# Query and key projection without padding, score banks read in pairs, and sums spread over the gaps, in a kernel of three attention blocks

## The chip, the cores and the metric

The kernel runs on one core of a Trainium2 chip. The metric is the device time in microseconds (us). A profile of one execution stands beside the timed runs; its times are microseconds from the start of the span, unless marked ns. TensorE multiplies matrices (PE in the profile, PEld for its weight loads), VectorE is DVE, ScalarE is ACT, GpSimd is POOL, and SyncE (SP) issues most of the transfers.

## What is computed

Input `x` has 4 sequences of 512 tokens with 288 features; a condition vector per sequence gives shifts, scales and gates. Three transformer blocks follow one another: block 0 with a mixture of four experts, block 1 with a dense part, then a rotation of a 64-dimensional subspace, then block 3 with a dense part. All is float32. The attention is the same in all three: 16 heads of 18 features.

```python
qkv = (h @ w_qkv + b_qkv).reshape(B, N, 3, nh, hd).transpose(2, 0, 3, 1, 4)
q, k, v = (qkv[0], qkv[1], qkv[2])
attn = jax.nn.softmax(jnp.einsum('bhqd,bhkd->bhqk', q, k) * hd ** (-0.5), axis=-1)
o = jnp.einsum('bhqk,bhkd->bhqd', attn, v).transpose(0, 2, 1, 3).reshape(B, N, C)
x = x + g_msa[:, None, :] * (o @ w_proj + b_proj)
```

Block 3 has no bias on q, k and v. After each attention come a second normalisation and the experts or the dense part (288 to 1152 to 288).

## The kernel before, in words

**Stages.** The code runs `attention(0)`, the experts, `attention(1)`, a dense part, `rotate()`, `attention(3)`, a dense part (L2018 to L2053). In the profile the tiles of the attentions begin with `a0`, `a1` and `a3`. Beside the attentions and the experts run background pieces, a step per `tick()` (L770): reflections (an orthogonal basis, on VectorE with small transfers `v<-pT`), a matrix exponential, and the routing of tokens to experts.

**Groups.** One attention is 16 groups `r` of one sequence and four heads (L786). Heads are padded from 18 to 32 rows, so the four heads of a group fill the 128 partitions of a query tile `qks[r, 0]` and a key tile `qks[r, 1]`. The weights come padded from the host; `queries_and_keys` (L829) multiplies padded weight columns with the activations `hT` (two full feature chunks and a remainder of 32 rows), one bank for the queries and one for the keys, and ScalarE adds the bias on the way out (L856). The key bias holds a 1 in row 18 of each head and the query row 18 is 0.

**Scores twice.** `row_max` (L862) makes the scores of 128 query tokens of one head with all 512 keys in a PSUM bank, and VectorE reduces them to the row maximum (L873). When a group has all its maxima, `shift` (L913) transposes them on TensorE and subtracts them from the query tile: row 18 of each head is then minus the maximum, which the 1 in the key's row 18 adds to every score. `weight` (L875) makes the scores again, transposed and shifted, and ScalarE takes Exp (L885). `sums` (L898) multiplies these with the values, which carry a column of ones, into one bank `av`; a key tile of 128 tokens is four products, one for each head.

**Gaps.** The order of TensorE is written out by hand: `mm` (L75) ties each product to the one before. A group runs through eight gaps `k` (L1143). A gap starts with `quad` (L888): two row-maximum products of group `r` and two weight products that lag nine gaps behind, on the four different 32-row strips of the array. Then come listed background steps, the sums (two key tiles in gap 1, two in gap 5, L1147 to L1152), and pieces of jobs by a string per gap (`pieces`, L1042): Q is a product of the next group's projection, A a block of transposed activations for the next sequence, X a values or output product. The last gap ends with `shift`. Groups 3, 4, 13 and 14 have no X. The first group's maxima run in four opening rounds (L1130).

**Banks and buffers.** PSUM has eight banks: four of tag `sc` for scores, three of tag `de` for everything else, and `av` (L64). The banks of the score ring come round in the order of `quad`, so a row-maximum bank is used again in the next gap, after its maximum has been read. Query and key tiles are rings of three, weights `p` a ring of ten (L1107). `Feed.hidden` (L1253) uses the score banks in the dense and expert parts: four remainder products into four banks, then the main ones.

**Transfers.** `collect` (L943) spreads a group's sums over partitions with copies on POOL's queue (L962) and one on SP (L957); `invert` (L964) sends the reciprocals on SP. Weights of an attention are loaded by `attention_weights` (L238): for block 0 at the program's start, for block 1 during the experts, for block 3 after attention 1. `Experts.loads` (L1441) lists copies of the expert weights in DRAM, issued from attention 0. `beside_of` and `in_turn` (L98, L102) order an instruction after the last one that was recorded for its engine; apart from such ties an engine's order is set by a scheduler from what is ready.

## Time and profile before

| what | value |
|---|---|
| median of 3 runs | 2056.34 us (2051.73 to 2058.46) |
| profiled execution | 2033.07 us |
| its span, first to last instruction | 2031.4 us |
| mean granted TensorE clock | 0.983 |
| attention 0, first score product to last sums | 29.9 to 412.9 |
| attention 1, the same | 936.9 to 1303.0 |
| attention 3, the same | 1507.5 to 1865.6 |
| VectorE busy in 80 to 386 (attention 0) | 222.7 of 306 |
| VectorE busy in 1507 to 1845 (attention 3) | 208.5 of 338 |

How to read the lines: a group line has the code line, the engine, the operation, written tile and read tiles, shapes and count; then busy time, the mean of one in ns, and the engine's idle time just before, with what ended it. In a timeline line stand the start, the length, the engine, the line, the operation and the count that was merged; `[0.76 <-DVE max L873]` is idle time and what ended it. A float32 product appears as two instructions, so one score product is two MATMUL records. Matmul lengths overlap in the pipeline, so the distance between starts is what one costs.

### The profile page before, as it was taken

What the parts mean: (1) busy time and instruction counts of PE and PEld (TensorE: products, weight loads), DVE (VectorE), ACT (ScalarE), POOL (GpSimd) and SP (SyncE); (2) the same over time, 40 slices, a digit from 0 to 9 for tenths busy, and PEclk for the clock granted to TensorE, in tenths of its full rate; (3) what the DMA queues carried; (4) which work ended last, traced back from release to release, by engine and by line L of the source; (5) the groups of instructions that cost most, each with busy time, mean ns of one, the idle gap of its engine ahead of it and who ended that gap; (6) DMA issues with size and microseconds to landing.
All of it is one profiled execution on the core that took longest, in us unless ns stands there. A gap on an engine that the chain in (4) does not pass through costs nothing.

```text
span 2031.4 us, 29536 instructions
## 1 busy us (share of the span) xinstructions
PE 1957.2 (96%) x10932; PEld 1045.6 (51%) x10932; DVE 1074.3 (53%) x3103; ACT 765.4 (38%) x1409; POOL 569.2 (28%) x803
## 2 busy tenths in 40 slices
PE   7999999999999999999999999999999999999998
PEld 4434444466667777776434443456654344433565
DVE  5666777623454333446777877454255556554211
ACT  1545555333312232322555544421125455555220
POOL 3111221443434446651332122211401111213101
PEclk9989999899999999999999999999999899999999
DMA  7421111447655766751112111220000111111000
GB/s 152 119 52 20 23 33 34 106 121 222 180 155 163 223 191 206 220 183 30 45 42 43 33 39 40 47 69 19 21 1 10 28 29 35 28 27 23 18 16 22
DMA packets 95698, 155.89 MB, mean 77 GB/s; under 512 B 33571, under 2 KB 71310, under 8 KB 95554
## 3 DMA queue, kind: packets, MB, share of 16 engines
q0 software_dynamic: 28672, 89.90, 14.7%
q1 hardware_dynamic: 66770, 64.10, 13.8%
q8 instruction: 86, 1.41, 0.3%
q14 instruction: 58, 0.48, 0.1%
q10 hardware_dynamic: 112, 0.01, 0.0%
HBM read 125.29 MB, written 18.48 MB: 71 GB/s over the span
## 4 chain that ended last, share of the span: by engine, by line
PE 70%; DVE 7%; DMA 4%; POOL 1%; issue 1%; ACT 1%; SPq 0%; POOLq 0%; DVEq 0%; ACTq 0%
PE e0h L76 9%; PE e0o L76 8%; PE a3m L76 7%; PE a1m L76 6%; PE av L76 6%; PE a3psqk L76 4%; PE f1h L76 4%; PE f3h L76 4%; PE a1psqk L76 4%; PE f1o L76 3%; DVE max L873 3%; PE f3o L76 3%; DMA v<-pT 2%; DMA wr<-in_wrot 1%; PE a3psv L76 1%; PE a3pp L76 1%
## 5 line engine op out<-in xcount | busy, mean ns | idle before, releaser
L873 DVE TENSOR_REDUCE max<-a3m 128x1 f32<-128x512 f32 x256 | 164.6, 686 | 132.9 <-PE a3s L76 122.3
L76 PE MATMUL e0h<-e0hT,e0w 128*128 128x256 f32 (+1 forms) x1188 | 229.0, 404 | 4.9 <-DMA e0w<-w1c,wrow 4.2
L873 DVE TENSOR_REDUCE max<-a0m 128x1 f32<-128x512 f32 x256 | 165.3, 683 | 94.3 <-PE a0s L76 81.7
L873 DVE TENSOR_REDUCE max<-a1m 128x1 f32<-128x512 f32 x256 | 165.8, 684 | 75.0 <-PE a1s L76 68.4
L76 PE MATMUL e0o<-e0w,e0hm 128*128 128x288 f32 x756 | 201.6, 417 | 0.0
L76 PEld LDWEIGHTS e0h<-e0hT,e0w 128*128 128x128 f32 (+1 forms) x1188 | 166.2, 189 | 62.3 <-issue 37.1
L885 ACT ACTIVATE a0p<-a0s 128x512 f32<-128x512 f32 x256 | 140.2, 596 | 146.8 <-PE a0s L76 146.7
L885 ACT ACTIVATE a1p<-a1s 128x512 f32<-128x512 f32 x256 | 140.9, 596 | 142.4 <-PE a1s L76 142.1
L885 ACT ACTIVATE a3p<-a3s 128x512 f32<-128x512 f32 x256 | 140.0, 596 | 139.2 <-PE a3s L76 139.1
L76 PE MATMUL a1m<-a1qk,a1qk 32*128 32x512 f32 x512 | 159.2, 647 | 8.0 <-DVE max L873 6.9
L76 PE MATMUL a0m<-a0qk,a0qk 32*128 32x512 f32 x512 | 159.4, 647 | 6.4 <-DVE max L873 5.3
L76 PEld LDWEIGHTS e0o<-e0w,e0hm 128*128 128x128 f32 x756 | 141.9, 192 | 42.5 <-issue 4.0
L76 PE MATMUL a0s<-a0qk,a0qk 32*128 32x512 f32 x512 | 160.4, 655 | 1.3 <-DVE max L873 1.3
L76 PE MATMUL a1s<-a1qk,a1qk 32*128 32x512 f32 x512 | 159.8, 647 | 0.2 <-DVE u L547 0.2
L76 PE MATMUL a3m<-a3qk,a3qk 32*128 32x512 f32 x512 | 152.1, 647 | 6.8 <-DVE max L873 5.5
L76 PE MATMUL a3s<-a3qk,a3qk 32*128 32x512 f32 x512 | 153.5, 647 | 0.3 <-DVE a3qk L927 0.3
L1279 ACT ACTIVATE e0hm<-e0h,e0w 128x256 f32<-128x256 f32 x189 | 89.5, 473 | 166.7 <-PE e0h L76 166.7
L607 POOL TENSOR_TENSOR nrm<-n,phalf 64x1 f32<-64x1 f32 (+31 forms) x64 | 36.6, 573 | 297.9 <-DVE n L604 294.1
L1813 ACT COPY e0r<-e0o 128x288 f32<-128x288 f32 x44 | 17.5, 398 | 184.1 <-PE e0o L76 176.4
L76 PEld LDWEIGHTS a1m<-a1qk,a1qk 32*128 32x128 f32 x512 | 47.4, 184 | 72.8 <-DVE max L873 44.1
L76 PEld LDWEIGHTS a0m<-a0qk,a0qk 32*128 32x128 f32 x512 | 47.4, 185 | 67.9 <-DVE max L873 38.8
L76 PE MATMUL f1h<-f1hT,w 128*128 128x512 f32 (+1 forms) x216 | 80.8, 614 | 0.4 <-ACT f1hT L502 0.4
(465 smaller groups left out, 3270.0 us busy)
## 6 DMA issues: line engine op xcount, KB each, us to landing
eo<-e0r SPq DMA_DIRECT2D x44, 144.0 KB
ada<-in_ada SPq DMA_DIRECT2D x18, 324.0 KB
wr<-in_wrot SPq DMA_DIRECT2D x16, 288.0 KB
g<-gates SPq DMA_DIRECT2D x24, 144.0 KB
w1c<-in_w SPq DMA_DIRECT2D x20, 144.0 KB
w<-in_w SPq DMA_DIRECT2D x6, 432.0 KB
x<-in_x SPq DMA_DIRECT2D x16, 144.0 KB
w1c<-in_w SPq DMA_DIRECT2D x8, 288.0 KB
```

Of the source, the lines that this page charges most:

```text
L76: ins = nc.tensor.matmul(*args, **kwargs).ins
L607: in_turn("POOL", nc.gpsimd.tensor_tensor(nrm, n2, phalf[0:n], ALU.pow))
L873: take("DVE", nc.vector.tensor_reduce(m[:, t, i, D : D + 1], ps, AX.X, ALU.max))
L885: take("ACT", nc.scalar.activation(p, ps, AF.Exp, scale=D**-0.5))
L1279: nc.scalar.activation(self.hms[i][f], ps[r][:, 0 : self.width], func, bias=b1(f)),
L1813: take("ACT", nc.scalar.copy(y, ps))
```

## The change

- **Projection.** Weights hold 576 columns without padding, ordered head by head with the query and the key of a head side by side. A column chunk is seven units of 18 (126 columns), five chunks per sequence. `queries_and_keys` makes one chunk per group (two where the next group is a sequence's first), in halves of 256 tokens and two `de` banks, into a tile `u`. Then eight transfers, four on SP for the queries and four on POOL for the keys, copy each head's 18 rows to its padded place.
- **Tiles.** The three query and three key tiles stay for the whole attention; POOL sets them at its start. Since the query's row 18 still holds an old maximum, `row_max` reads 18 rows, and `shift` multiplies by a mask before it subtracts.
- **Weights.** For block 0 the padded weights are loaded to other tiles and ScalarE copies them together. For blocks 1 and 3 twelve transfers in attention 0 compact them in DRAM. The bias goes through DRAM in three transfers that depend on one another.
- **Scores.** The score banks are two tiles of two banks. Two heads' scores go to one tile, and one reduction or one Exp reads both banks. `hidden` takes its banks in the same way.
- **Order.** One key tile is summed in gap 3, 5, 7 and in gap 1 of the next group but one; the strings are written anew; the first half of the first sequence's values is made before the opening rounds.

```diff
+UC = HC * D
+NU = -(-2 * H // HC)
...
-    banks = {"sc": 4, "de": 3}
-
     def bank(tag, name):
-        return psum.tile([P, 512], F32, tag=tag, name=name, bufs=banks[tag])
+        return psum.tile([P, 512], F32, tag=tag, name=name, bufs=3)
+
+    def two_banks(name):
+        return psum.tile([P, 2, 512], F32, tag="sc", name=name, bufs=2)
...
+    mask = cst.tile([P, 1], F32, tag="mask", name="mask")
+    nc.vector.tensor_reduce(mask, ident[:, D::DP], AX.X, ALU.add)
+    nc.vector.tensor_scalar(mask, mask, -1.0, 1.0, ALU.mult, ALU.add)
...
+        def step(l, k, n):
+            to = compact[l][:, k, :].rearrange("p (h s d) -> s p h d", s=2, d=D)[n]
+            src = a[f"wqk{l}"][:, k, n * NG * P : (n + 1) * NG * P]
+            src = src.rearrange("p (h e) -> p h e", e=DP)[:, :, 0:D]
+            beside_of("SP", nc.sync.dma_start(to, src))
+
+        return [
+            lambda l=l, k=k, n=n: step(l, k, n)
+            for l in (1, 3)
+            for k in range(KC)
+            for n in range(2)
+        ]
...
+        def biases():
+            load(w["bqk"], a[f"bqk{l}"])
+            wide = dram.tile([2 * NG * P], F32, tag=f"bw{l}", name=f"bw{l}")
+            load(wide.rearrange("(j p) -> j p", p=P), a[f"bqk{l}"].rearrange("p j -> j p"))
+            flat = dram.tile([2 * C], F32, tag=f"bu{l}", name=f"buf{l}")
+            load(
+                flat.rearrange("(h s d) -> h s d", s=2, d=D),
+                wide.rearrange("(s h e) -> h s e", s=2, e=DP)[:, :, 0:D],
+            )
+            full = 2 * C // UC
+            load(w["bu"][:, 0:full], flat[0 : full * UC].rearrange("(c p) -> p c", p=UC))
+            load(w["bu"][0 : 2 * C - full * UC, full:NU], flat[full * UC :].unsqueeze(1))
...
         def qk():
-            load(w["bqk"], a[f"bqk{l}"])
-            full_chunks(w["qk"], a[f"wqk{l}"])
+            biases()
+            if compact:
+                full_chunks(w["qk"], compact[l])
+                return
+            for n in range(2):
+                t = wt.tile([P, W1R], F32, tag="w1", name=f"wide{l}_{n}", bufs=4)
+                t = t[:, 0 : MC * NG * P].rearrange("p (m n) -> p m n", m=MC)
+                full_chunks(t, a[f"wqk{l}"][:, :, n * NG * P : (n + 1) * NG * P])
+                heads = t.rearrange("p m (h e) -> p m h e", e=DP)
+                for m in range(MC):
+                    o = apart(w["qk"], n)
+                    in_turn("ACT", nc.scalar.copy(o[:, m], heads[:, m, :, 0:D]))
...
             def queries_and_keys(r):
...
+                b, g = groups[r]
+                for c in range(g + 1 if g else 0, g + 2):
+                    yield
+                    m = min(UC, 2 * C - c * UC)
+                    cols = slice(c * UC, c * UC + m)
+                    ps = [bank("de", f"{name}psqk{r}_{c}_{k}") for k in range(2)]
+                    tokens = [slice(k * T // 2, (k + 1) * T // 2) for k in range(2)]
+
+                    def product(k, n, rows):
+                        mm(
+                            ps[k][0:m, 0 : T // 2],
+                            lhsT=w["qk"][:, n, cols] if n < MC else w["qkr"][rows, cols],
+                            rhs=hTs[b][rows, n, tokens[k]],
+                            start=(n == MC),
+                            stop=(n == MC - 1),
+                        )
+
+                    for k in range(2):
+                        product(k, MC, slice(k * RR, (k + 1) * RR))
+                    u = us[b, c] = pool.tile([P, T], F32, tag="u", name=f"{name}u{r}_{c}")
+                    for k in range(2):
+                        for n in range(MC):
+                            yield
+                            product(k, n, slice(0, P))
+                        nc.scalar.activation(
+                            u[0:m, tokens[k]],
+                            ps[k][0:m, 0 : T // 2],
+                            AF.Identity,
+                            bias=w["bu"][0:m, c : c + 1],
+                        )
+
+                for i in range(GH):
+                    for s, queue in ((0, nc.sync), (1, nc.gpsimd)):
+                        c, row = divmod(2 * (g * GH + i) + s, HC)
+                        o = qks[r, s][i * DP : i * DP + D, :]
+                        queue.dma_start(o, us[b, c][row * D : (row + 1) * D, :])
+
+            def heads_rows(i, n=DP):
+                return slice(i * DP, i * DP + n)
+
+            def row_max(r, t, i):
+
+                m = maxima[r % 2].rearrange("p t (h d) -> p t h d", d=DP)
+                ps = two_banks(f"{name}m{r}_{t}_{i}")
+                for k in range(2):
+                    mm(
+                        ps[:, k, :],
+                        lhsT=qks[r, 0][heads_rows(i + k, D), t * P : (t + 1) * P],
+                        rhs=qks[r, 1][heads_rows(i + k, D), :],
+                        start=True,
+                        stop=True,
+                    )
+                    yield
+                take(
+                    "DVE",
+                    nc.vector.tensor_reduce(m[:, t, i : i + 2, D], ps, AX.X, ALU.max),
+                )
...
+            def weight(r, t, i):
+                s = two_banks(f"{name}s{r}_{t}_{i}")
+                for k in range(2):
                     mm(
-                        ps[s],
-                        lhsT=w["qkr"][rows, g * P : (g + 1) * P],
-                        rhs=hTs[b][rows, MC, :],
+                        s[:, k, :],
+                        lhsT=qks[r, 1][heads_rows(i + k), t * P : (t + 1) * P],
+                        rhs=qks[r, 0][heads_rows(i + k), :],
                         start=True,
-                        stop=False,
+                        stop=True,
                     )
...
-                p = pool.tile([P, T], F32, tag="p", name=f"{name}p{r}_{t}_{i}", bufs=tags["p"])
-                take("ACT", nc.scalar.activation(p, ps, AF.Exp, scale=D**-0.5))
-                return p
+                    yield
+                p = pool.tile([P, 2, T], F32, tag="p", name=f"{name}p{r}_{t}_{i}", bufs=tags["p"])
+                take("ACT", nc.scalar.activation(p, s, AF.Exp, scale=D**-0.5))
+                for k in range(2):
+                    ps[r, t, i + k] = p[:, k, :]
+                yield
...
+                halves = [what(r, n // 2, n % 2 * 2) for what, r, n in halves]
+                for _ in range(3):
+                    for half in halves:
+                        next(half)
...
                 q = qks[r, 0]
-                take("DVE", nc.vector.tensor_sub(q, q, ps))
+                take(
+                    "DVE",
+                    nc.vector.scalar_tensor_tensor(q, q, mask, ps, ALU.mult, ALU.subtract),
+                )
...
-                pieces = {0: "QQ", 2: "QQQ", 3: "QQQ", 4: "XQX", 6: "XX", 7: "X"}
+                pieces = {0: "QQ", 1: "Q", 2: "QQ", 4: "XX", 5: "X", 6: "XX"}
+                if g == NG - 1:
+                    pieces = {0: "QQQ", 1: "Q", 2: "QQQ", 3: "Q", 4: "QQ", 5: "X", 6: "XXX", 7: "X"}
...
-                    pieces = {0: "QQA", 2: "QQQ", 3: "QQQ", 4: "QAA", 6: "XXX", 7: "XX"}
+                    pieces = {0: "QQQ", 1: "Q", 2: "QA", 3: "A", 4: "A", 5: "XX", 6: "XXX"}
...
-            tags = {"qk0": 3, "qk1": 3, "p": 10}
+            tags = {"p": 5}
+            n, gaps = len(groups), 2 * NT
...
+            for k in range(3):
+                for s in range(2):
+                    t = pool.tile([P, T], F32, tag=f"qk{s}_{k}", name=f"{name}qk{s}_{k}", bufs=1)
+                    if s == 0:
+                        nc.gpsimd.memset(t, 0.0)
+                    else:
+                        nc.gpsimd.tensor_copy(t, w["bqk"][:, NG : NG + 1].to_broadcast([P, T]))
+                    for r in range(k, n, 3):
+                        qks[r, s] = t
...
-            first = [queries_and_keys(0)]
+            first = [queries_and_keys(0), values(0, 0)]
...
-            jobs["X"], jobs["Y"] = values(0, 0), values(0, 2)
+            jobs["X"] = values(0, 2)
...
-            for t, pieces in enumerate(("QQQQ", "QQQQQ", "XXXXX", "YYYYY")):
+            for t, pieces in enumerate(("QQ", "QQQ", "XX", "XXX")):
...
                     if k == 1 and r > 1:
-                        sums(r - 2, 2)
-                        sums(r - 2, 3)
-                    if k == 5:
-                        sums(r - 1, 0)
-                        sums(r - 1, 1)
+                        sums(r - 2, NT - 1)
+                    if k % 2 and k > 1:
+                        sums(r - 1, k // 2 - 1)
...
-                if k == 0:
-                    sums(n - 2, 2)
-                    sums(n - 2, 3)
+                if k == 1:
+                    sums(n - 2, NT - 1)
...
-            ps = [bank("sc", f"{self.name}h{i}_{f}") for i, f in chunks]
+            ps = []
+            for k in range(0, len(chunks), 2):
+                two = two_banks(f"{self.name}h{chunks[k][0]}_{chunks[k][1]}")
+                ps.extend(two[:, n, :] for n in range(2))
...
-            got = [lambda: features(self.wg[:, :, 0:E], a["wgate"])]
+            got = [lambda: features(self.wg[:, :, 0:E], a["wgate"])] + compacting()
```

## The prediction

> **What bounds the kernel now.** First the page's busy line, then the groups, then the timeline of a few gaps, because an average over the span does not say which wait ends last.
>
> ```profile
> PE 1957.2 (96%) x10932; PEld 1045.6 (51%) x10932; DVE 1074.3 (53%) x3103; ACT 765.4 (38%) x1409; POOL 569.2 (28%) x803
> ...
> L873 DVE TENSOR_REDUCE max<-a3m 128x1 f32<-128x512 f32 x256 | 164.6, 686 | 132.9 <-PE a3s L76 122.3
> ...
> L76 PE MATMUL a3m<-a3qk,a3qk 32*128 32x512 f32 x512 | 152.1, 647 | 6.8 <-DVE max L873 5.5
> ```
>
> TensorE is busy almost throughout, and the score products wait only 5.5 us for the maxima in the whole third attention. I call the work from one block of four score products to the next a gap; a group of four heads has eight, numbered 0 to 7. The timeline of gap 2 in group 2 of the third attention (start, length in us):
>
> ```profile
> 1553.99 0.69 PE L76 MATMUL a3m<-a3qk,a3qk 32*128 32x512 f32 x1
> ...
> 1555.06 1.56 PE L76 MATMUL a3psqk<-a3hT,wqk 128*128 128x256 f32 x6
> 1555.14 1.29 DVE L873 TENSOR_REDUCE max<-a3m 128x1 f32<-128x512 f32 x2 [1.27 <-PE a3s L76]
> ...
> 1556.55 0.69 PE L76 MATMUL a3m<-a3qk,a3qk 32*128 32x512 f32 x1
> ```
>
> The four score products share the array and take 1.07 (1553.99 to 1555.06), three projection pieces 1.49, so 0.497 each, and the gap is their sum, 2.56: TensorE-bound. The same reading gives 0.92 for the sums of one key tile, 0.585 for a values or output product, 0.87 for the shift's four transposes. A gap with nothing to fill it shows the second bound:
>
> ```profile
> 1583.12 0.69 PE L76 MATMUL a3m<-a3qk,a3qk 32*128 32x512 f32 x1
> ...
> 1584.28 1.29 DVE L873 TENSOR_REDUCE max<-a3m 128x1 f32<-128x512 f32 x2 [2.21 <-PE a3s L76]
> ...
> 1585.02 0.69 PE L76 MATMUL a3m<-a3qk,a3qk 32*128 32x512 f32 x1 [0.76 <-DVE max L873]
> ```
>
> Products to maximum 1.16, the first maximum 0.686, release to the next product 0.06: 1.90. This loop is the floor of a gap, because a score bank is filled again one gap later; the other gaps lie above it.
>
> **The change, part by part.**
>
> Projection (gain on TensorE). A group needs 8 pieces of 0.497 and a pair of remainder products (0.96): 4.94 us, 79 per attention. After: five column chunks per batch, each 4 pieces and a remainder pair half as long (0.48): 2.47 each, 49 per attention. So 30 us of TensorE time go per attention, 89 in all. That is the gain only if nothing else ends the gaps.
>
> Paired banks (new floor). One maximum now reads two banks, and the next pair of products needs both. The trace has no such read. A VectorE read of 256 columns from PSUM takes 418 ns, one of 512 686: 1.047 ns a column, so 1.22 for 1024. Bounds: 1.07 (the slope alone) and 1.37 (two old ones); the slope's value is nearest to its rows, so I take 1.22. The floor rises from 1.90 to 1.16 + 1.22 + 0.06 = 2.44. The paired Exp, 596 ns plus 427 more at ScalarE's slope (687 for 512 columns, 473 for 256), is 1.02: its loop, 2.25, lies under VectorE's.
>
> Sums in every other gap. Nothing is saved; 1.84 in gaps 1 and 5 becomes 0.92 in gaps 1, 3, 5, 7. An ordinary group (third attention, group 6) measures 2.55, 2.91, 2.56, 2.56, 2.66, 2.91, 2.24, 2.76 = 21.2. After: gaps 0 and 2 hold 1.07 + 0.98, under the floor, 2.44; gap 1 1.07 + 0.92 + 0.5 = 2.49; gaps 3, 4, 6 2.44; gap 5 2.58; gap 7 with the shift 2.86: 20.1. TensorE's own work in it would be 18.6, and the floor holds five gaps up by 1.5 in all, so 1.1 of the saving arrives. The other kinds, in the same way: with activations 22.0 to 21.3; with two chunks 21.4 to 21.2 (20.8 to 20.3 without output products); without values 20.7 to 19.9. Over groups 1 to 14 of the third attention: 12.5 us.
>
> The first two attentions have other VectorE work, 111 and 113 us against 48 (reflections, routing). VectorE's free time in a 2.44 gap is 2.44 - 1.22 = 1.22, and a step of the reflections takes about 1.3. From score product to score product their groups 1 to 14 already take 310 and 306 against the third's 299 (4 us of a clock event left out of the first and the third). To the third's new 287 I add one and a half times that excess, 303 and 297: gains 7 and 9. Sum of the gaps: **-28.5**.
>
> Copies to padded tiles (new wait). Per group four copies on SP and four on POOL, like `oo<-raw` (0.51 to issue on POOL, 1.9 to land) and `den<-raw` (0.63 on SP): 2.5 + 1.9 = 4.4 after the last bias. In a running group they start after gap 2 (gap 4 with two chunks), 12 us (8) ahead: cost 0, cover gone only if SP stands still that long. POOL gets 2.1 us more a group, with 57 to 85 us busy in 306 to 353: hidden. At an attention's start they are bare: 4.4 later than the 5.55 from the first projection (931.37) to the first score product (936.92). POOL also sets six tiles there (three memsets of 0.52, three copies at the 0.8 of a 288-column add or more), queued ahead of its key copies: 1. The values' first half moves into this wait, and the four opening rounds, bound by VectorE (16 x 0.686 = 11.0 becomes 8 x 1.22 = 9.8), lose 1 to 3. Net +3 for the second and third attention: **+6**.
>
> First attention's start. The chain now is:
>
> ```profile
> 5.79 0.36 SPq L252 DMA_DIRECT2D bqk<-in_bqk  x1
> ...
> 6.83 1.97 SPq L178 DMA_DIRECT2D wqk<-in_wqk  x4
> ...
> 28.26 9.03 SPq L173 DMA_DIRECT2D x<-in_x  x12
> ```
>
> SP issues without a break to 37 us, and the first projection (21.13) waits for these loads. After, three transfers that depend on each other (bias to DRAM, compacted, back) stand ahead of the weights on SP: 2 us of landing each if SP must wait, nothing if its order lets the weights pass; six ScalarE copies (0.40 each) follow the load. Then the query copies need SP among the `x` loads. Bounds 0 and 20; taken 5 for the first group, 2 for the second's copies, 2 for the twelve weight compactions (1536 runs each; 384 runs of 12 bytes passed in about 1 us, so 4 us each, in bursts of up to four behind the normaliser's transfers): **+9**.
>
> Clock gate. The clock row halves without a long idle:
>
> ```profile
> 1584.20:1587.60 3.40, 2.34 (x16) 0.98 (x12) 2.58 (x4) 2.28 (x4) 0.00 (x0) 1.00 0.28 25
> 1587.60:1597.80 10.20, 10.20 (x39) 2.82 (x39) 4.37 (x9) 2.17 (x4) 0.00 (x0) 0.50 0.23 63
> ```
>
> Columns: stretch, length, then busy time of PE, PEld, DVE, ACT, POOL, granted clock, DMA share. Two thin gaps (0.76 and 0.30 idle) were enough; the next group took 25.4 instead of 21.4, so 4 us an event. The new schedule idles 0.3 to 0.4 in most gaps and 1.36 in gaps 4 and 6 of the four groups of an attention that have no values or output products. I take one more event than now: **+4**; bounds 0 and 12 events, 48.
>
> The Trainium skill ("TensorE: Matmul & The Clock Gate", section "Why this matters for your kernels") speaks of idle gaps above about 3 us between bursts as what costs the clock. By it these gaps cost nothing, and the sum would be 4 us lower; the row above shows the clock halved after 0.76, and the measurement decides.
>
> Dense and expert stages: `hidden` takes its banks in pairs, but its four remainder products always needed all four banks before the main ones: 0.
>
> Sum: -28.5 + 6 + 9 + 4 = -9.5 against the profiled 2033.07 (span 2031.4). That execution lies 23 under the median of 2056.34; I carry the difference over: **2047**, -0.5%. Within 0.3% (6 us) counts as no change, about what a measurement of this kernel can tell.
>
> **Rivals.**
>
> *Clock and floor (slower).* The thin gaps trip the gate. For: the event above and one at 113.0 in the first attention, both after a group without output products, and one at 1270.2 in the second's last group. Against: groups 13 and 14 have such gaps at 1.90 and tripped nothing. Place: gaps 4 and 6 of groups 3, 4, 13, 14 and the last group. Price 4 each. From 4 events beyond the one counted it is slower than before by 6; at 8 more in all, -28.5 + 15 + 32: 2075. A pair read of 1.37 does the same, 0.15 in five gaps of 45 groups, +34.
>
> *Copies late on SP (slower).* The twelve compactions stand in one burst, 48 us, and a group's query rows behind it; 12 are covered, up to 36 lost once: 2083. For: SP ran the expert weights' copies from 41 to 76 us in one go. Against: each waits in its turn behind a group's own transfers.
>
> *Starts eat it (no change).* The first start costs 15 instead of 5: 2057.
>
> *Full gain.* The starts and the clock cost nothing: 2028; with a read of 1.07, 34 less than forecast, 2013.
>
> *It does not pair.* If products of 18 rows did not share the array, a gap's block would pass 2 us; the sums of 19 columns share it today, so I give this nothing apart.
>
> **The numbers.** Forecast 0.40, full gain 0.10, no change 0.15, clock and floor 0.27, late copies 0.08. Faster 0.50, same 0.15, slower 0.35. Range 2012 to 2083: the read's two bounds and both slower cases at their prices.
>
> **What would show it.** Right: gaps 0, 2, 3, 4 and 6 near 2.44 in the third attention, product idle before them put down to the maximum; pair read near 1.22; query and key copies landed before a group's first product. Wrong: gaps of 2.1 (the floor does not hold); TensorE waiting on DMA at a group's start; more than three half-clock stretches inside attentions; a first score product after 45 us.

## The result, and the profile after

The changed kernel takes **2243.49 us** (median of 4 runs, 2236.13 to 2250.72); the kernel before, on the same chip, 2054.03 (4 runs, 2048.6 to 2058.46). Ratio 1.0924, 95% interval 1.0869 to 1.0978: slower by 9%, where 0.5% faster was forecast and 2083 was the upper end. In a second set of runs (after_again below) the ratio was 1.0793 (1.0725 to 1.0861). The kernel before had medians from 2033 to 2063 beside the runs below, so kernels are compared below by their ratio to before on the same chip.

First the page of the profile after: busy times, then groups (busy, mean ns of one, idle time of the engine ahead of them and what ended it).

```profile
PE 1961.3 (88%) x10692; PEld 960.8 (43%) x10692; DVE 1057.3 (47%) x2721; ACT 726.3 (33%) x1055; POOL 675.7 (30%) x1013
...
L79 PE MATMUL e0h<-e0hT,e0w 128*128 128x256 f32 (+1 forms) x1188 | 258.3, 419 | 61.8 <-ACT e0hm L1382 47.3
...
L951 DVE TENSOR_REDUCE max<-a3m 128x2 f32<-128x1024 f32 x128 | 156.6, 1226 | 125.6 <-PE a3s L79 122.3
...
L79 PE MATMUL a3m<-a3qk,a3qk 18*128 18x512 f32 x512 | 147.7, 654 | 29.5 <-DVE max L951 29.5
```

TensorE is busy about as long as before (1961 against 1957 us) in a span 203 us longer. The paired maximum takes 1.226 us: the price forecast. The score products now wait 29.5 us for it in the third attention (5.5 before): the floor. The first group is new: TensorE stands 47 us for ScalarE's reads of the experts' hidden products, in a stage that the prediction charged with nothing. The same group in the kernel before:

```profile
L76 PE MATMUL e0h<-e0hT,e0w 128*128 128x256 f32 (+1 forms) x1188 | 229.0, 404 | 4.9 <-DMA e0w<-w1c,wrow 4.2
```

Then the windows of four stages: the first attention from its first score product to its last block of them, the expert stage, and the same of the second and the third attention. Columns: stretch, length, busy times of PE, PEld, DVE, ACT and POOL with their counts, granted clock, DMA share, GB/s. The kernel before:

```profile
29.90:384.40 354.50, 345.07 (x2120) 148.63 (x2120) 257.69 (x648) 167.78 (x298) 71.77 (x114) 0.99 0.27 63
412.90:931.40 518.50, 497.81 (x3028) 365.20 (x3020) 202.82 (x936) 143.22 (x325) 246.90 (x277) 0.98 0.60 183
936.90:1281.20 344.30, 333.28 (x1994) 140.62 (x1994) 264.74 (x657) 165.54 (x290) 82.58 (x125) 0.99 0.17 38
1507.50:1843.90 336.40, 328.45 (x1996) 137.75 (x1996) 207.36 (x383) 164.69 (x290) 57.36 (x96) 0.98 0.12 25
```

The changed kernel:

```profile
57.50:442.50 385.00, 344.74 (x2022) 125.73 (x2022) 251.44 (x519) 154.52 (x186) 100.31 (x171) 0.88 0.33 68
471.70:1079.90 608.20, 525.77 (x3027) 361.05 (x3020) 203.63 (x936) 143.65 (x325) 247.61 (x277) 0.97 0.53 156
1087.80:1445.10 357.30, 318.38 (x1903) 112.93 (x1902) 259.12 (x530) 151.15 (x178) 112.72 (x185) 0.93 0.21 49
1689.40:2024.90 335.50, 306.02 (x1899) 110.03 (x1898) 201.41 (x257) 150.78 (x178) 86.15 (x154) 0.97 0.17 38
```

Three things stand there. The expert stage grew by 90 us at the same instruction counts. The first two attentions grew by 31 and 13 us at a clock of 0.88 and 0.93 instead of 0.99: TensorE has fewer products there, and a row-maximum product takes 732 and 687 ns in the mean instead of 647. Only the third attention, where the gaps were read for the prediction, did not grow (335.5 against 336.4 us); it was forecast to shrink by 12.5.

The stages of all profiles that the account below needs, worked out from the first and last matmuls of each tile, in us (the column names are those of the experiments):

| stage | before, twice | after, twice | across_again | filled2 | single_f2 |
|---|---|---|---|---|---|
| span's start to first projection | 21.1, 21.8 | 39.5, 39.2 | 39.0 | 24.2 | 24.9 |
| to first score product | 8.8, 8.6 | 18.0, 18.1 | 18.5 | 13.1 | 13.7 |
| first attention, score products | 354.5, 352.2 | 385.0, 368.6 | 375.6 | 361.1 | 352.0 |
| expert stage | 518.5, 533.0 | 608.2, 591.9 | 557.1 | 535.4 | 534.3 |
| second attention, projection to first score product | 5.5, 5.5 | 7.9, 7.9 | 7.9 | 9.1 | 8.2 |
| second attention, score products | 344.3, 346.4 | 357.3, 366.1 | 353.3 | 343.9 | 343.0 |
| dense stage of layer 1 | 195.5, 196.5 | 211.5, 211.2 | 195.5 | 196.3 | 197.1 |
| third attention, score products | 336.4, 331.5 | 335.5, 338.8 | 335.7 | 329.3 | 320.5 |
| dense stage of layer 3 and end | 165.8, 165.8 | 187.7, 187.9 | 169.9 | 169.3 | 169.2 |
| at half clock among score products | 27, 17 | 160, 151 | 131 | 21 | 21 |

### The profile page after: what moved, and what is told of

The parts are those of the page before. It is cut to its first block, busy times and chain, and to the rows that moved or that the text cites. A ratio compares the mean times of both kernels' runs of the same rounds, so it can differ in the third digit from the quotient of the medians.

```text
span 2234.4 us, 29755 instructions
## 1 busy us (share of the span) xinstructions
PE 1961.3 (88%) x10692; PEld 960.8 (43%) x10692; DVE 1057.3 (47%) x2721; ACT 726.3 (33%) x1055; POOL 675.7 (30%) x1013
## 3 DMA queue, kind: packets, MB, share of 16 engines
q1 hardware_dynamic: 95944, 71.78, 15.6%
## 4 chain that ended last, share of the span: by engine, by line
PE 63%; DVE 11%; ACT 4%; DMA 3%; issue 2%; SPq 0%; another core or an unknown queue 0%; POOL 0%; POOLq 0%; ACTq 0%; DVEq 0%
PE e0h L79 10%; PE e0o L79 8%; DVE max L951 7%; PE a3m L79 6%; PE a1m L79 5%; PE av L79 5%; PE f3h L79 4%; PE f1h L79 3%; PE f1o L79 3%; PE f3o L79 3%; ACT e0hm L1382 2%; PE a3psqk L79 2%; PE a1psqk L79 1%; PE a0m L79 1%; PE a3pp L79 1%
## 5 line engine op out<-in xcount | busy, mean ns | idle before, releaser
L951 DVE TENSOR_REDUCE max<-a3m 128x2 f32<-128x1024 f32 x128 | 156.6, 1226 | 125.6 <-PE a3s L79 122.3
L951 DVE TENSOR_REDUCE max<-a0m 128x2 f32<-128x1024 f32 x128 | 156.1, 1222 | 114.7 <-PE a0s L79 99.2
L79 PE MATMUL a0m<-a0qk,a0qk 18*128 18x512 f32 x512 | 164.0, 732 | 48.2 <-DVE max L951 30.4
L967 ACT ACTIVATE a0p<-a0s 128x1024 f32<-128x1024 f32 x128 | 130.7, 1024 | 209.6 <-PE a0s L79 209.6
L951 DVE TENSOR_REDUCE max<-a1m 128x2 f32<-128x1024 f32 x128 | 156.1, 1222 | 86.0 <-PE a1s L79 81.3
L967 ACT ACTIVATE a1p<-a1s 128x1024 f32<-128x1024 f32 x128 | 130.7, 1025 | 184.8 <-PE a1s L79 184.0
L79 PE MATMUL a1m<-a1qk,a1qk 18*128 18x512 f32 x512 | 155.6, 687 | 38.9 <-DVE max L951 37.3
L967 ACT ACTIVATE a3p<-a3s 128x1024 f32<-128x1024 f32 x128 | 130.7, 1025 | 166.8 <-PE a3s L79 166.8
L79 PE MATMUL a3m<-a3qk,a3qk 18*128 18x512 f32 x512 | 147.7, 654 | 29.5 <-DVE max L951 29.5
L79 PE MATMUL f3h<-f3hT,w 128*128 128x512 f32 (+1 forms) x216 | 83.6, 621 | 14.3 <-ACT f3hm L1382 10.3
L79 PE MATMUL f1h<-f1hT,w 128*128 128x512 f32 (+1 forms) x216 | 84.1, 622 | 12.6 <-ACT f1hm L1382 8.4
```

The costliest lines, as they stand in the source:

```text
L79: ins = nc.tensor.matmul(*args, **kwargs).ins
L951: nc.vector.tensor_reduce(m[:, t, i : i + 2, D], ps, AX.X, ALU.max),
L967: take("ACT", nc.scalar.activation(p, s, AF.Exp, scale=D**-0.5))
```

## The experiments

### The four chunks of hidden laid across the pairs

The prediction priced the dense and expert stages at 0, because a call of `hidden` needs all four banks anyway. That holds between calls. Inside a call the trace of after shows something else; one call, start and length in us:

```profile
743.34 1.77 PE L79 MATMUL e0h<-e0hT,e0w 32*128 32x256 f32 x12
...
745.15 0.47 ACT L1382 ACTIVATE e0hm<-e0h,e0w 128x256 f32<-128x256 f32 x1 [2.76 <-issue]
...
745.68 1.99 PE L79 MATMUL e0h<-e0hT,e0w 128*128 128x256 f32 x8 [0.56 <-issue]
...
747.71 0.47 ACT L1382 ACTIVATE e0hm<-e0h,e0w 128x256 f32<-128x256 f32 x1 [0.39 <-PE e0h L79]
...
748.24 1.13 PE L79 MATMUL e0h<-e0hT,e0w 128*128 128x256 f32 x4 [0.56 <-ACT e0hm L1382]
...
749.41 0.48 ACT L1382 ACTIVATE e0hm<-e0h,e0w 128x256 f32<-128x256 f32 x1 [1.22 <-PE e0h L79]
```

The main products stop twice, before the second and the fourth chunk, each time until ScalarE has read the chunk ahead (745.15 + 0.47 = 745.62, next product 745.68), though that chunk lies in the other bank of the pair. Before the third, in the other pair, there is no stop. The edit lays each chunk beside one that is two further on:

```diff
-            for k in range(0, len(chunks), 2):
-                two = two_banks(f"{self.name}h{chunks[k][0]}_{chunks[k][1]}")
-                ps.extend(two[:, n, :] for n in range(2))
+            pairs = [two_banks(f"{self.name}h{i}_{f}") for i, f in chunks[0:2]]
+            ps.extend(pairs[k % 2][:, k // 2, :] for k in range(len(chunks)))
```

> The changed kernel, but the four chunks of a call of hidden are laid across its two pairs of banks (chunks 0 and 2 in the first, 1 and 3 in the second), so that no chunk follows the one that shares its pair. Theory (waits follow the pair, not the bank: the second chunk's products stand until ScalarE has read the first chunk): the expert stage goes back from 608 to about 520 us, the two stretches of the dense stages from 211 and 188 to about 195 and 166, in all 128 us less than the changed kernel: about 2115 (2105 to 2130). Rival (the stages behind the attentions are longer because of more DMA traffic or a lower clock): no change, 2243.

Measured: 2147.38, ratio 1.0416 (1.0349 to 1.0483). The dense stages fell to 195.4 and 169.9, as the theory said. The expert stage came to 563 only, on a chip whose kernel before took 2062.57; there `e0h` still stood 25.7 us, 15.6 of them for `e0hm`, so the new layout does not end every such wait. So both kernels were run on one more chip.

> The changed kernel once more, unchanged, on the same chip as the next run: 2215 to 2250. It is the reference for the size of hidden's term.

> The run across once more, on the same chip as the changed kernel. If hidden's pairs cost what the stages of the first two profiles say (expert stage 90, dense 16 and 22), it is 120 to 130 us faster than the changed kernel there; if part of those 128 us was the chip's longer expert stage, 85 to 110.

Measured: 2205.25 (1.0793) and 2124.29, ratio 1.0417 (1.0360 to 1.0474). The difference is 81 us (76 by the ratios, with some 18 either way). By stages it is 16 and 18 in the dense ones and 35 in the expert stage, where across_again had 65 us at half clock and after_again 24, so that the 35 are a low figure. The layout cost about 80, not 128 (with the ratio of the first set of runs the step would be 104); what else lengthened the expert stage comes below (before_again, laid). TensorE's idle time ahead of hidden's products gives a size apart from the half-clock time; after_again, then across_again:

```profile
L79 PE MATMUL e0h<-e0hT,e0w 128*128 128x256 f32 (+1 forms) x1188 | 250.7, 411 | 51.9 <-ACT e0hm L1382 47.4
L79 PE MATMUL e0h<-e0hT,e0w 128*128 128x256 f32 (+1 forms) x1188 | 234.8, 410 | 5.9 <-DMA e0w<-w1c,wrow 4.1
```

That is 46 us; the two dense stages add 12.6 and 14.3 against 0.7 and 0.7, so 71 in all. A call in across_again, with the same instructions:

```profile
741.74 4.37 PE L79 MATMUL e0h<-e0hT,e0w 32*128 32x256 f32 x24
...
743.55 0.47 ACT L1381 ACTIVATE e0hm<-e0h,e0w 128x256 f32<-128x256 f32 x1 [1.31 <-PE e0h L79]
744.41 0.47 ACT L1381 ACTIVATE e0hm<-e0h,e0w 128x256 f32<-128x256 f32 x1 [0.39 <-PE e0h L79]
...
746.14 0.47 ACT L1381 ACTIVATE e0hm<-e0h,e0w 128x256 f32<-128x256 f32 x1 [0.39 <-PE e0h L79]
```

The products run through: 741.74 to 746.11, against 743.34 to 749.37 in after, 1.66 us less in this call. The same four banks take the same four chunks in the same order of work, only paired otherwise, so the wait follows the pair, not the bank. The Trainium skill ("PSUM — Partial Sum Buffer", section "PSUM bank collisions raise a hardware error") asks for PSUM to be guarded by bank and quadrant, by bank in its simple version; this program's wait went by the pair, twice as coarse, and the 1.66 us are what that costs in the call shown.

### Parts of the change alone

`single` takes the pairs back and leaves the rest: four banks as before, one maximum and one Exp a bank.

```diff
+    banks = {"sc": 4, "de": 3}
...
-                ps = two_banks(f"{name}m{r}_{t}_{i}")
                 for k in range(2):
+                    ps = bank("sc", f"{name}m{r}_{t}_{i}_{k}")
...
-                    nc.vector.tensor_reduce(m[:, t, i : i + 2, D], ps, AX.X, ALU.max),
+                        nc.vector.tensor_reduce(m[:, t, i + k, D : D + 1], ps, AX.X, ALU.max),
```

> The changed kernel with single banks everywhere: scores, maxima, exponentials and hidden as in the kernel before; unpadded projection, copies and sums in every other gap stay. Theory (the pairs cost the most, through hidden and through the floor of 2.47 us a gap, which leaves TensorE short idle times that lower its clock): hidden's 128 us go, gaps fall to TensorE's own 2.0 to 2.5 us, some 2 us less in each of 45 groups than before (-90), against +28 to +34 of the starts: 1990 to 2020. Rival (the copies and the unpadded projection cost the time: late tiles, thin gaps, clock): at least 2085, which is before plus the starts.

Measured: 2117.13, ratio 1.0273 (1.0233 to 1.0312). The expected gain is not there; the rival was right on the time. Its third attention did shorten, to 323.7, but its start is 37.7 and 18.9, and its score products spend 123 us at half clock; both are taken apart below.

`pairs` is the opposite: the kernel before with paired banks alone.

```diff
-                ps = bank("sc", f"{name}m{r}_{t}_{i}")
+                ps = two_banks(f"{name}m{r}_{t}_{i}")
...
-                take("DVE", nc.vector.tensor_reduce(m[:, t, i, D : D + 1], ps, AX.X, ALU.max))
+                    nc.vector.tensor_reduce(m[:, t, i : i + 2, D], ps, AX.X, ALU.max),
```

> The kernel before with paired banks alone: pairs for scores, maxima and exponentials, hidden laid across its pairs; padded projection, no copies, sums as before. Theory (a pair's floor of 2.47 us binds only where a gap holds less; with the padded projection most gaps hold 2.5 or more): third attention's groups 21.2 to 22, the gaps of 1.9 become 2.47, in all +15 to +35: 2070 to 2090, few more stretches at half clock. Rival (the pairs by themselves bring the lower clock of the changed kernel's first two attentions): 2100 and more.

Measured: 2094.23, ratio 1.0178 (1.0123 to 1.0233), +32 on its chip: the upper part of the theory's range. Groups 1 to 14 of the third attention take 301.8 against 298.6 in the second profile of before, their thin gaps 2.47 instead of 1.90; half-clock time among score products is 38 us, not 131 or more. So the pairs alone do not bring the low clock. Against that profile groups 1 to 14 account for some 12 of the 32 (8, 1 and 3 in the three attentions); in its expert stage of 567 `e0h` stood 26.9 us, 13.0 of them for `e0hm`, where sums on the same chip had 6.5 in all. So the range held, but part of the time came from the stage that the theory did not name.

`sums` is the kernel before with only the sums moved.

```diff
-                        sums(r - 2, 2)
-                        sums(r - 2, 3)
-                    if k == 5:
-                        sums(r - 1, 0)
-                        sums(r - 1, 1)
+                        sums(r - 2, NT - 1)
+                    if k % 2 and k > 1:
+                        sums(r - 1, k // 2 - 1)
```

> The kernel before with the sums of one key tile in gaps 1, 3, 5 and 7 instead of two in gaps 1 and 5; nothing else. Theory (the same TensorE work, and TensorE bounds the gaps): within 8 us of before, 2046 to 2062. Rival (the spread leaves the gaps with two tiles' sums shorter than VectorE's two maxima and others longer): 2065 and more.

Measured: 2077.96, ratio 1.0108 (1.0060 to 1.0157): the rival. Gap 3, with three projection pieces and now a sum, takes 3.55 instead of 2.56, gap 2 takes 3.00, and gaps 1 and 5 give back less than that (2.06 instead of 2.91); an ordinary group takes 21.71 instead of 21.17. The order of the sums pays only with the thinner list of pieces that the change gives it.

The expert stage of `sums` was 551, and nothing in it was edited:

> The kernel before once more, unchanged, for a second profile. The run with the sums alone moved had its expert stage at 551 us against 518 in the first profile of before, though nothing in that stage was edited. If the first profile caught a short expert stage, this one shows 530 to 550 there and the other stages within 5 us of the first; if the sums' order really lengthens the expert stage, it shows 518 again.

Measured: 2042.38 (one run). Its expert stage is 533.0, every other stage within 5 us of the first profile. The first profile of before caught a short expert stage. That stage moves by itself, and in part with the clock: 518.5 with 17 us at half clock, 533.0 with 37, and in the last run below (before_fill, which edits nothing there) 556 with 65; but sums has 551 with the same 37, so the clock is not all of it. One profile of it says little; where the account needs it, medians are used.

### The weights and biases laid ready

The change makes unpadded weights and biases on the chip. SP's queue at the start, in the changed kernel:

```profile
7.13 0.77 SPq L282 DMA_DIRECT2D bw<-in_bqk  x1
7.94 3.25 SPq L185 DMA_DIRECT2D wide<-in_wqk  x3
20.17 0.60 SPq L282 DMA_DIRECT2D buf<-bw  x1
20.81 1.68 SPq L185 DMA_DIRECT2D wide<-in_wqk  x3
23.88 0.84 SPq L282 DMA_DIRECT2D bu<-buf  x2
```

Three weight transfers pass, then SP stands from 11.19 to 20.17, until the 4 KB of the first bias transfer have landed, 13 us after their issue, and everything behind it is late. In `laid` the host lays both:

```diff
         def qk():
             biases()
-            if compact:
-                full_chunks(w["qk"], compact[l])
-                return
...
+            full_chunks(w["qk"], a[f"wqkc{l}"])
...
+        both = np.stack([w.reshape(C, H, D) for w in (wq, wk)], 2)
+        a[f"wqkc{l}"] = _chunks(both.reshape(C, 2 * C))
```

> The run across, but the host lays the query and key weights without padding and the biases by column chunks, beside the padded ones: the chain of three dependent bias transfers, ScalarE's six copies and the twelve compactions in the first attention go; nothing else changes. Theory (SP stands for the chain, and its compactions hold the loads of ada back until TensorE waits): first projection at 22 to 28 us instead of 38.9, the first attention 5 to 10 us shorter from first to last score product: 15 to 30 us less than across, 2117 to 2132. Rival (the first group waits for its query copies behind the loads of x in any case, and the compactions were hidden): within 6 us of across.

Measured: 2096.81, ratio 1.0302 (1.0277 to 1.0326), against 1.0417 of across: 23 us, in the theory's range. The first projection starts at 24.5 instead of 38.9. But the attention did not shorten (372.9); the other part came from a stage that the forecast did not name. The expert stage is 528.8, where across had 563 and 557. SP's queue in that stage of across_again shows why:

```profile
605.53 0.72 SPq L282 DMA_DIRECT2D bw<-in_bqk  x1
606.30 6.08 SPq L185 DMA_DIRECT2D wqk<-wqkc  x2
622.26 0.57 SPq L282 DMA_DIRECT2D buf<-bw  x1
622.87 1.22 SPq L185 DMA_DIRECT2D wqk<-wqkc  x2
629.04 0.83 SPq L282 DMA_DIRECT2D bu<-buf  x2
629.91 0.86 SPq L606 DMA_DIRECT2D v<-pT  x1
```

The second attention's chain runs in the expert stage, with 10 and 5 us of standing (612.38 to 622.26 and 624.09 to 629.04), and `v<-pT`, which the reflections wait for, and the experts' results are queued behind it. The wait can be followed to TensorE (`m` is a step of the matrix exponential, which stands behind `v` in VectorE's order):

```profile
633.48 0.14 DVE L610 COPY v<-v 42x1 f32<-42x1 f32 x1 [14.68 <-DMA v<-pT]
635.89 1.01 PE L765 MATMUL pst<-m,nskew 64*64 64x64 f32 x8 [14.44 <-DVE m L789]
```

All five profiles with the chain in this stage (after, after_again, across, across_again, single) have this wait of TensorE for `m`, 9.2 to 14.4 us at the longest; in the other profiles it is at most 0.9. So 14 us of the 28 are the chain's. The twelve Gelus over which it lies (ScalarE's reads of hidden's products, the 49th to the 61st of the stage) agree: 54 us in across_again, 53 in across, 40 in laid, 38 in third. The rest goes with half-clock time, which differs too (65 and 37).

`laid_q` also sends the first group's query copies on ScalarE's queue, and fills the key tiles' padding from a column made on the chip:

```diff
-                    for s, queue in ((0, nc.sync), (1, nc.gpsimd)):
+                    for s, queue in ((0, nc.sync if r else nc.scalar), (1, nc.gpsimd)):
...
-                        nc.gpsimd.tensor_copy(t, w["bqk"][:, NG : NG + 1].to_broadcast([P, T]))
+                        nc.gpsimd.tensor_copy(t, pad.to_broadcast([P, T]))
```

> The run laid, and two more edits at an attention's start: the first group's query copies go out on ScalarE's queue instead of behind the loads of x on SP, and the padded key tiles are filled from a column made on the chip, so that POOL does not wait for the biases. Theory (queue order sets the start): from the first projection to the first score product of the first attention about 10 us instead of 18.9, and the projection itself up to 10 earlier: 8 to 18 us less than laid. Rival (the copies' own time of 4.4 us and the transposes set it): within 4 us of laid.

Measured: 2088.93, ratio 1.0276 (1.0230 to 1.0322): 5 us, not to be told from nothing. From projection to first score product it is 13.9 instead of 18.3 in the profiles, and the projection starts no earlier: behind the weights, the normaliser's transposes wait for VectorE. Less than forecast; the two edits, not tried apart, were worth 4 of the 9 us.

### The clock

Stretches at half clock begin in after without a long wait. The opening rounds of its second attention:

```profile
1095.78 1.62 PE L79 MATMUL a1m<-a1qk,a1qk 18*128 18x512 f32 x8
1097.23 1.34 PE L79 MATMUL a1psv<-wv,a1hT 32*128 32x288 f32 x6
1098.89 3.08 PE L79 MATMUL a1m<-a1qk,a1qk 18*128 18x512 f32 x8 [0.32 <-DVE max L951]
1101.90 3.25 PE L79 MATMUL a1psv<-wv,a1hT 128*128 128x288 f32 x6
```

```profile
1100.20:1120.70 20.50, 20.27 (x64) 8.87 (x67) 12.39 (x29) 5.29 (x7) 2.36 (x4) 0.50 0.02 7
```

For 20.5 us the clock (the last column but two) is 0.50. In the 10 us before, the longest idle time of TensorE is the 0.32 shown. The Trainium skill ("TensorE: Matmul & The Clock Gate", section "Why this matters for your kernels") names idle gaps above about 3 us; no such gap is here, and the measurement decides. What the change altered is how much goes through the array: the opening rounds have 10 pieces where before they had 19, and the running gaps hold fewer projection pieces. `filled` tests that by putting the work back as products that nothing reads:

```diff
+            def fill(k, taken):
+                us = 1.07 + 0.92 * (k % 2) + 0.5 * taken + (0.87 if k == gaps - 1 else 0)
+                m = int((2.45 - us) / 0.25)
+                if m > 0:
+                    idle = bank("de", f"{name}idle")
+                    for _ in range(m):
+                        mm(idle[:, 0:128], lhsT=ident, rhs=ones, start=True, stop=True)
```

> The run laid_q, with products of 128 columns that nothing reads put into every gap whose planned TensorE work is under 2.45 us, as many as fit. They add work and no result. Theory (gaps with idle TensorE lower the granted clock, and that is most of what the attentions lose): the time at half clock inside the three attentions falls from about 147 us in across to under 50, which is worth half of the difference, 40 us or more, and the fillers cost under 15: 20 to 45 us less than laid_q. Rival (VectorE's late maxima make the long gaps, and the clock only follows them): no gain, 0 to 15 us more than laid_q.

Measured: 2062.39 against 2088.93 on the same chip, ratio 1.0113 (1.0089 to 1.0137): 26 us less, inside the theory's range. Half-clock time among score products is 82 us (133 in laid_q), not under 50; what is left in the profile is mostly the openings.

```diff
                 work_off(jobs, pieces)
+                fill(0, len(pieces), 1.15)
                 if t % (NT // ticks) == 0:
```

(The last argument is added to the 2.45 us.)

> The run filled, with such products also in the four opening rounds of each attention, up to 3.6 us of TensorE work a round (the change left two or three pieces there instead of four or five). Theory (the stretches of 20 us at half clock that start in the opening rounds come from idle TensorE there): they go, 8 to 10 us in each of the first two attentions and up to 5 in the third: 1.13% over before in filled becomes 0.0 to 0.4%. Rival (the stretches come from something else at the start, or the fillers delay the rounds): as filled, within 0.3%, or slower.

Measured: 2059.55, ratio 1.0106 (1.0063 to 1.0149): no further gain in the medians, so on that the rival holds. The profiled execution, though, has none of these stretches in the second and third attention (filled's profiled execution was its slowest, 14 us over the median, so it had more of them than most). Its three attentions:

```profile
37.30:398.40 361.10, 344.70 (x2244) 149.40 (x2244) 252.37 (x519) 154.22 (x186) 101.39 (x171) 0.97 0.30 72
965.30:1309.20 343.90, 329.19 (x2148) 142.80 (x2148) 258.33 (x529) 150.86 (x178) 111.27 (x183) 1.00 0.22 50
1535.60:1864.90 329.30, 326.20 (x2149) 142.16 (x2148) 201.32 (x257) 150.69 (x178) 86.30 (x154) 1.00 0.18 39
```

The same three in laid_q:

```profile
38.20:405.50 367.30, 333.37 (x2024) 121.35 (x2024) 252.26 (x519) 154.24 (x186) 101.59 (x171) 0.92 0.29 70
962.20:1317.60 355.40, 314.79 (x1899) 111.67 (x1898) 260.14 (x530) 150.91 (x178) 112.38 (x185) 0.94 0.21 49
1545.10:1883.90 338.80, 310.07 (x1899) 111.31 (x1898) 201.31 (x257) 150.66 (x178) 86.29 (x154) 0.95 0.17 37
```

With 110 to 125 products more in each (220 to 250 records, two for a product), every attention is shorter than in laid_q, the clock 1.00 in two of them. Together the two fillings give 35 us (1.0276 to 1.0106): adding work saved time.

The control asks whether fillers help any kernel of this shape:

```diff
                     work_off(jobs, pieces.get(k, ""))
+                    fill(1.07 + 1.84 * (k in (1, 5)), jobs, pieces.get(k, ""))
                     if k == gaps - 1:
```

Its text counts half-clock time with the attentions' last rounds, where the changed kernel has 179 us (the 197 in the text is a slip):

> The kernel before with products that nothing reads in its own thin gaps (up to 2.05 us of planned TensorE work a gap, also in the last rounds of an attention); nothing else. It is the control for filled2 and single_f2: if fillers pay only where the change had thinned the gaps, before gains nothing here, within 0.3%, because it has 41 and 27 us at half clock inside its attentions in two profiles, against 197 in the changed kernel's first. If fillers make any kernel of this shape faster, 0.5% or more faster.  Rival on the other side: the fillers stand ahead of score products and cost 0.3% or more.

Measured: 2057.87 against 2059.07, ratio 0.9993 (0.9964 to 1.0022): nothing. So fillers do not help every kernel of this shape; here they give back what the change took.

### The parts put together

`single_q` has the edits of single, laid and laid_q; `single_f2` adds `fill` with 2.05 in place of 2.45, and 3.5 us in the opening rounds.

> The run single (unpadded projection and copies, one bank at a time), with the mended start of laid_q. Theory (the start's terms add to the banks' independently): single's 2.7% over before less the 1.4% that laid and laid_q gained together: 1.1 to 1.5% over before; time at half clock still above 80 us inside the attentions, because gaps of 1.9 to 2.1 us hold little TensorE work. Rival (with single banks the start's waits were hidden): 2% or more over before.

Measured: 2064.18, ratio 1.0121 (1.0079 to 1.0163), with 123 us at half clock: as expected.

> The run single_q, with products that nothing reads in every gap under 2.05 us of planned TensorE work and in the opening rounds up to 3.5 us. Theory (the clock is what is left): half-clock time inside the attentions falls below 50 us and the groups of the third attention stay near 20 us against 21.2 before: 0.3 to 1.2% faster than before. Rival (VectorE sets the gaps of the first two attentions, and the clock follows): 0 to 1% slower than before.

Measured: 2043.75, ratio 1.0048 (1.0023 to 1.0072): the rival's side, though the half-clock time (21 us) and the third attention's groups (20.0) are the theory's. Groups 1 to 14 take 308.1, 303.6 and 288.7 us in the three attentions, against 309.5, 311.0 and 298.6 in the second profile of before (306.3 in the second attention of the first profile, with no half-clock time there). Against the gains stand longer starts (3 us to the first projection, 5 more to the first score product, 3 in the second attention) and 3.4 us more between the last matmul and the span's end (12.2 to 12.5 against 8.7), which every run with the unpadded projection in all three attentions shows, and whose cause stays open. The spans of these two profiles are about equal (2039.0 and 2040.7), so they do not show where the 10 us of the timed runs lie.

The last run asks for a version that beats both kernels: only the third attention changed.

```diff
+            thin = l == 3
...
-                    jobs["Q"] = queries_and_keys(r + 1)
+                    jobs["Q"] = (queries_and_keys if thin else padded_qk)(r + 1)
```

(`padded_qk` is the projection of the kernel before; the pieces, the sums, the start and the fillers are chosen by `thin` in the same way.)

> The kernel before in its first two attentions; the third alone takes the unpadded projection with copies, the weights laid by the host, one bank at a time, sums of one key tile in every other gap, and the filling products, as in single_f2. Theory (VectorE has little else to do in the third attention, so there the saved TensorE time arrives: 320.5 us from first to last score product in single_f2 against 331.5 and 336.4 in two profiles of before; the other two attentions gain nothing): 8 to 12 us less than before, less up to 3.4 us that single_f2's end of the span was longer: 0.2 to 0.6% faster. Rival (the copies load SP and POOL so that the start of the third attention or the dense stage behind it gives it back): within 0.2%.

Measured: 2036.42 against 2033.15, ratio 1.0016 (0.9986 to 1.0047): no difference to be seen, so the rival's number held, though not visibly for its reason (the start takes 8.8 against 9.0, the dense stage behind it is no longer). Its third attention took 326.8, with 13.7 us at half clock right behind the opening rounds; the first two attentions, which are as before, had 44 us at half clock among their score products, against 17 in each profile of before. No version here beats the kernel before.

## Why the prediction was wrong, point by point

The account of the difference of 161 us on the chip of after_again, by steps of ratio (times 2033; the medians there differ by 172): hidden's layout 76 (81 by the medians); weights and biases made on the chip 23; order of the copies 5, not certain; clock 35; paired against single banks 12 (filled2 to single_f2); left over 10, in a place that the profiles do not show. The first step is taken on one chip, the second between two, the others on a third; each is good to some 10 us, the first to 18. The first set of runs had 190 us. Its profile has a mean clock of 0.947 against 0.956 in after_again, and its first attention and expert stage are 16 us longer each; why its clock was lower is not shown.

- **Dense and expert stages, "0": the step that failed, 76 to 81 us (71 of them seen as idle time ahead of hidden's products).** The argument that the four remainder products always needed all four banks is true between two calls. It did not ask what stands between the second chunk's products and the first chunk's Gelu inside a call. The rule the prediction itself used for the scores, that a pair is released as a whole, applied here too.
- **First attention's start, "+9" within 0 to 20: too small, its bounds too, and not complete.** The stages show +18 to the first projection and +9 more to the first score product. The bounds gave SP's standing 2 us a landing; the first bias transfer took 13. The chain of the second attention in the expert stage was not seen at all, though it stands on the same queue. By the ratios the terms are 23 and 5 us, the chain in the expert stage among them. The compactions, taken at 2, do show in one place (in group 5 of the first attention TensorE stands up to 2.0 us for `ada`, whose loads come late), but runs with and without them don't separate that.
- **Clock gate, "+4" within 0 to 48: too small.** The mechanism of the rival *Clock and floor* was right, its place only in part: the stretches start in the thin gaps it named, and also in the opening rounds and where VectorE's reflections and routing delay a maximum. 35 us came back with fillers. The count of events was read off the kernel before and moved by one, though the change takes half of the pieces out of the opening rounds and a good part of those in the gaps.
- **Gaps, "-28.5": mechanism right, size wrong.** The pair read was 1.226 (1.22 forecast), the floor 2.47 (2.44). Gaps 4 and 5 of group 4 of the third attention in after:

```profile
1782.77 0.69 PE L79 MATMUL a3m<-a3qk,a3qk 18*128 18x512 f32 x1 [0.35 <-DVE max L951]
...
1785.24 0.69 PE L79 MATMUL a3m<-a3qk,a3qk 18*128 18x512 f32 x1 [1.33 <-DVE max L951]
...
1787.71 0.69 PE L79 MATMUL a3m<-a3qk,a3qk 18*128 18x512 f32 x1 [0.35 <-DVE max L951]
```

2.47 apart, the wait put down to the maximum, 1.33 idle in gap 4 (1.36 forecast): the mechanism is there. But with the clock at 1.00, groups 1 to 14 of the third attention take 296.2 (filled2) against 298.6: 2.4 gained, not 12.5. A gap with a sum and a product takes 2.74, where 2.49 to 2.58 was worked out, and the groups with two chunks 22.06 instead of 21.2. In the first two attentions the gain is none (315.1, with 10 us at half clock, and 307.6, against 309.5 and 306.3 in the profiles of before without half-clock time there). So about 26 of the 28.5 us did not arrive.
- **Starts of the second and third attention, "+6": the sum came out, not its parts.** From first projection to first score product it is 2.4 us more in the second attention, 0.7 more or 1.0 less in the third. The opening rounds with their shift, forecast to lose 1 to 3, took 1.4 to 2.8 us longer, partly at half clock. That makes 6.3 in one profile and 6.9 in the other, by luck.
- **Carry-over from the profiled execution to the median:** the profile of before lay 23 us under the median it was compared with, and its expert stage alone was 15 us shorter than in the second profile; nothing says that such a difference carries over to another kernel.

No rival held the result. *Clock and floor* had its sign and ended 168 us short, because the largest term was in a stage that none of them touched. Three signs of being wrong that the prediction named did show (first score product at 57.5, 10.0 us of waiting for the copies `a0qk<-a0u` there, 20 half-clock stretches in the attentions where more than three was the sign); none of them points at that stage.

## What to carry to other kernels

When two buffers become one, walk through every user of the old ones and ask of each instruction whether it now waits for a reader of the other half; a part that is used one half at a time should take its halves from different pairs. A transfer that depended on a transfer held its whole queue here until the landing (9 us at the start, 10 and 5 in the expert stage), so price such a one by what is queued behind it, in whichever stage it runs. And when TensorE work is removed from a loop that another engine bounds, look at the granted clock before counting the gain.

## What the runs showed of the hardware that was not expected

- TensorE's clock fell to 0.50 for 20.5 us with no idle time over 0.32 us in the 10 us before; 110 to 125 added products an attention (filled2) brought its mean from 0.92, 0.94 and 0.95 to 0.97, 1.00 and 1.00, and took 6 to 12 us off each attention of laid_q.
- The bias transfer, 4 KB whose 1024 words are turned one by one, held what depends on it for 13 us at the start and 17 in the expert stage, where the prediction's row, `oo<-raw` of 36 KB, landed in 1.9.
- The time of an unedited stage differs from run to run, and only in part with the clock: the expert stage of before took 518 to 556 us with 17 to 65 us at half clock, and with 37 it took 533 in before_again, 551 in sums.
